# Indirect gathers issued behind TensorE's and ScalarE's work, and the first scores of an attention unit issued behind the slot's other TensorE products

## The chip, the cores and the metric

One core of a Trainium2 chip runs the whole program. The metric is device time in microseconds (us) of one execution. Before the change the median of four runs is 15278.71 us (15266.43 to 15290.21).

## The reference, cut to what matters

```
x = x + conv(gn(x))                    # two mamba layers, along time and along variables
t = tokens(x)                          # (4, 3072, 256) = 12288 tokens
n = layernorm(t)
h = tanh(q[:, :, None, :] + k[:, None, :, :] + bh)      # q, k: 32 numbers a token
e = einsum('biju,u->bij', h, Wa) + ba                   # "scores"
t = t + softmax(e) @ n                                  # attention inside each of 4 batches
n2 = layernorm(t)
g = n2 @ W_gat                                          # 4 heads x 4 experts
a_src, a_dst = (g * att_src).sum(-1), (g * att_dst).sum(-1)
alpha = softmax over each token's incoming edges of leaky_relu(a_src[src] + a_dst[dst])
s = layernorm(segment_sum(g[src] * alpha, dst))         # gates: top 2 of 4 experts
t = t + sum over experts e of gate_e * (gelu(n2 @ W1[e] + b1[e]) @ W2[e] + b2[e])
```

The edge list has 1048576 entries, given as indices up to 65535. Of these only the ones that point at a real token count; the kernel sorts them out itself and then fetches the rows of their sources and targets from two tables in device memory (`tab_s`, 20 numbers a row, and `tab_a`, 4 numbers a row).

## The kernel before, in words

**Engines and order.** The kernel writes out by hand the order of the instructions of TensorE (PE), ScalarE (ACT), VectorE (DVE) and GpSimd (POOL). Each of these runs its own list strictly in that order and waits where an input or a buffer is not ready. DMAs are issued by SyncE (SP), except the indirect gathers, which POOL issues.

**Layer 0.** `Layer0.run` (L566 on) yields twice a slot, 48 slots a block of 384 columns. In each slot it emits decays on ACT (L384), scans on DVE (L401), products with the output matrix C on POOL (L408, L415 to L417), and for the next block the TensorE products px (L214), pd (L262), pt (L283) and pz (L458). These products share one PSUM buffer, `pp`; a product can start when VectorE has read the one before it out.

**Attention.** `Attention.units` (L778 on) runs interleaved with it, one slot at a time. Each slot emits one tanh over 3072 keys (L814; 3072 of them in all, into one of three `th` buffers), lets the other work emit its first half, emits the scores of the tanh of two slots before (L787), lets the other work emit its second half, and then does one step of the tail of the unit before. Eight slots make a unit of 32 queries; the eight score calls of a unit add into one PSUM buffer `pe`. After the eighth, VectorE takes the maximum (`nb`, L868) and ScalarE the exponential (`pr`, L875), which frees `pe`. The first scores of the next unit (k = 0) therefore wait for `pr`. The steps of the unit's tail follow in the next slots: two transposes (L882) and the values (L891); every fourth unit also a `spread` on POOL (`sf`, L950) and a product `together` (L955).

**Beside attention.** `steps` in `whole` gives out the second stream: layer 0 while it lasts (with some expert work in `Beside`, L1522 and L1533), then `Edges.sort` on VectorE with its TensorE products `pc` (L1216), then `Experts.early` (L1608 and L1616). When the sort has ended, two gathers of `tab_a` rows a slot are issued (`Edges.gather`, L1037) for the first three of four batches: 324 gathers of 128 rows.

**Tail.** `tail` (L1709 on) runs when attention is over. It is a list of steps t. Three steps make one expert unit (512 tokens, one expert): products `ph` (L1608), four gelus (L1690), products `po` (L1616). 37 units remain there. Among the steps stand the 36 groups of 12 edge columns: `Graph.gather` (432 gathers of `tab_s`, L1314, and the last 108 of `tab_a`), `scores` (L1331 to L1335), `spread` (L1350, L1354) and `place` (products `pa`, L1364). Group m has its scores at step 10 + 5m/2, its places up to four steps later. After the last group of a batch `finish` turns the sums into gates. Each of the 24 kept blocks of 512 tokens is then weighted and stored, at least four steps apart and not before its batch's `finish` (`half`: 16 additions on VectorE, L1693; `all`, 2 MB, `y` and `out`, 0.5 MB each, by SP).

These lines of `tail` set the steps:

```
t = G0 + PART * m // 2
at(max(0, t - 10), lambda j=j: gr.gather(j))
at(t, lambda j=j: gr.scores(j))
```

The buffers that matter: `gs` 4, `h1` (gelu's output) 2, `ko` (a unit's output) 2, `all` and `y` 2 each.

Of the kernel before, what the change touches and what calls it, by code (L numbers as in the profile page):

```python
# [26 lines left out]
P = 128  # L27
# [32 lines left out]
G1, K1 = 8, 4  # L60
GP, GG = 12, 4
EDGE_US = 2.4
G0, PART = 10, 5
KO_BUFS = 2
SLOT_US, PRODUCT_US = 1.2, 0.11
EU, EG = 32, 2
# [572 lines left out]
class Attention:  # L639
# [4 lines left out]
    def __init__(self, ctx, tc, ident, a, x1, x2, xn2T, tab_s, tab_a):  # L644
        self.nc = nc = tc.nc
        self.ident, self.x1, self.x2, self.xn2T = ident, x1, x2, xn2T
        self.tab_s, self.tab_a = tab_s, tab_a
        pool = lambda name, bufs, **k: ctx.enter_context(
            tc.tile_pool(name=name, bufs=bufs, side="right", **k))
        const = self.const = pool("atc", 1)  # L650
        self.rows, self.th, self.wk = pool("atr", 2), pool("atb", TH_BUFS), pool("atw", 1)
        self.ps_e = pool("ate", PE_BUFS, space=PSUM)
        self.ps_v = pool("atv", PV_BUFS, space=PSUM)

        def load(name, shape, ap):
# [24 lines left out]

        self.later = []

    def psum(self, name):
        return self.ps_v.tile([P, JB], F32, tag="pv", name=name)
# [90 lines left out]
    def units(self, side):  # L775
# [24 lines left out]
        while i < B * PER + LAG or todo or self.later:  # L800
# [10 lines left out]
            if b < B:  # L811
                s = self.state[b]
                th = self.th.tile([P, TOK], F32, tag="th", name="th")
                nc.scalar.activation(th, s["krep"], AF.Tanh, bias=s["qsel"][:, col:col + 1])  # L814
                behind.append(th)
            yield
            late, self.later = self.later, []
            for f in late:
                f()
            busy = tail = None  # L820
            if behind and i >= LAG:
                n, k = divmod(i - LAG, NK)
                if k == 0:
                    pe = self.ps_e.tile([P, 2, JB], F32, tag="pe", name="pe")
                scores(pe, k, behind.pop(0))
                if k == NK - 1:
                    tail = self.unit_tail(*divmod(n, TOK // QU), pe)
                    busy = True

            self.extra = 0.0 if tail or not todo else getattr(todo[0], "us", 0.0)  # L830
            yield
            if tail:

                for f in todo:
                    f()
                todo = tail()
            elif todo and hasattr(todo[0], "us"):
                if not todo[0].full:
                    beside()
                todo.pop(0)()  # L840
                busy = True
            elif todo:
                todo.pop(0)()
# [167 lines left out]
class Edges:  # L1011
# [3 lines left out]

    def __init__(self, ctx, tc, a):
        self.nc, self.tc, self.a, self.todo = tc.nc, tc, a, []
        keep = ctx.enter_context(tc.tile_pool(name="el", bufs=1))  # L1020
        new = lambda name, shape, dt=F32: keep.tile(shape, dt, tag=name, name=name)
        self.cnt = new("cnt", [P, NH])
        self.lost = new("lost", [P, 1])
        self.si, self.di = new("si", [P, 4, CQ], I32), new("di", [P, 4, CQ], I32)
        self.lane, self.tile = new("lane", [P, 4, CQ]), new("tile", [P, 4, CQ])
        self.lanes, self.tiles = new("lanes", [P, P]), new("tiles", [P, NH])
        self.nc.sync.dma_start(self.lanes, a["lanes"])

    def places(self, pool, tab_a):

        self.gd = pool.tile([P, 4, CQ, HEADS], F32, tag="gd", name="gd")
        self.tab_a, self.have = tab_a, set()

    def gather(self, q, c):
        if (q, c) not in self.have:
# [57 lines left out]
    def sort(self):  # L1093
# [4 lines left out]
        with ExitStack() as ctx:  # L1098
# [73 lines left out]
            v.tensor_scalar(hi, flat(x3), 7, None, ALU.logical_shift_right)  # L1172
            v.tensor_copy(flat(self.lane), lo)
            v.tensor_copy(flat(self.tile), hi)
            yield 1.5


# [11 lines left out]
            v.tensor_copy(l4, self.lanes.unsqueeze(2).to_broadcast([P, P, K1]))  # L1189
            v.tensor_copy(t4, self.tiles.unsqueeze(2).to_broadcast([P, NH, K1]))  # L1190
            yield 1.0
            p = ctx.enter_context(tc.tile_pool(name="eo", bufs=3))
            ps = ctx.enter_context(tc.tile_pool(name="ep", bufs=1, space=PSUM))
            pc = ps.tile([P, NH], F32, tag="pc", name="pc")
            starts = [q * W2 + g for q in range(4) for g in range(0, C1, G1)]

            def one_hots(c0):
                hot = []
                for name, table, of, n in (("ol", l4, lane, P), ("oh", t4, tile, NH)):
                    t = p.tile([P, G1 // K1, n, K1], BF16, tag=name, name=name)  # L1200
                    which = of[:, c0:c0 + G1].rearrange("p (g k) -> p g k", k=K1)
                    v.tensor_tensor(t, table.unsqueeze(1).to_broadcast([P, G1 // K1, n, K1]),
                                    which.unsqueeze(2).to_broadcast([P, G1 // K1, n, K1]),
# [1 line left out]
                    hot.append(t)  # L1205
                return hot

            ahead = one_hots(starts[0])
            yield G1 * (P + NH) / 1800
            for i in range(len(starts)):  # L1210
                hot, ahead = ahead, one_hots(starts[i + 1]) if i + 1 < len(starts) else None

                def products(i=i, hot=hot):
                    for u in range(G1):
# [13 lines left out]
class Graph:  # L1228
# [4 lines left out]
    def __init__(self, ctx, tc, a, ed, tab_s, tab_a, gates):  # L1233
# [5 lines left out]
        self.bg, self.lg, self.lb = (self.load(a, k, HF) for k in ("bg_rep", "lg_rep", "lb_rep"))  # L1239
        self.eps = self.new("eps2", [P, 1])  # L1240
        self.nc.vector.memset(self.eps, 1e-5)
        self.got, self.v, self.pa = {}, {}, {}

    def new(self, name, shape):
        return self.const.tile(shape, F32, tag=name, name=name)
# [59 lines left out]
        nc.vector.tensor_tensor(wl, wl, ed.cnt.unsqueeze(2).to_broadcast([P, NH, ROW]), ALU.mult)  # L1305
        nc.vector.tensor_tensor(acc, acc, wl, ALU.add)

    def gather(self, j):
        nc, ed = self.nc, self.ed
        gs = self.wk.tile([P, GP, ROW], F32, tag="gs", name="gs", bufs=4)  # L1310
        q, c0 = divmod(j * GP, CQ)
        rows = self.tab_s.rearrange("p n f -> (p n) f")
        for u in range(GP):
            nc.gpsimd.indirect_dma_start(  # L1314
                out=gs[:, u, :], out_offset=None, in_=rows,
                in_offset=bass.IndirectOffsetOnAxis(ap=ed.si[:, q, c0 + u:c0 + u + 1], axis=0))
            ed.gather(q, c0 + u)

        for c in range(4 * j, min(4 * j + 4, CQ)):
            ed.gather(3, c)  # L1320
        self.got[j] = gs

    def scores(self, j):
        nc = self.nc
        gs = self.got.pop(j)
        q, c0 = divmod(j * GP, CQ)
        gd = self.ed.gd[:, q, c0:c0 + GP, :]
        e = self.wk.tile([P, GP, HEADS], F32, tag="e", name="e")
# [377 lines left out]
def tail(tc, a, ed, ex, w, tab_s, tab_a, gates):  # L1706


    with ExitStack() as ctx:  # L1709
# [11 lines left out]
            at(2 * n, lambda: next(own, None))  # L1721
        hot, ready = {}, {}
        PQ = CQ // GP
        for m in range(4 * PQ):
            j = m
            t = G0 + PART * m // 2
            if m < 1:
                gr.gather(j)
            else:
                at(max(0, t - 10), lambda j=j: gr.gather(j))  # L1730
            at(t, lambda j=j: gr.scores(j))
            for g in range(GP // GG):
                at(t + 1 + g, lambda j=j, g=g: hot.update({(j, g): gr.spread(j, g)}))
                at(t + 2 + g, lambda j=j, g=g: gr.place(j, g, *hot.pop((j, g))))
# [36 lines left out]
        for t in range(max(3 * len(units) + 3, end)):  # L1771
# [3 lines left out]
            if n < len(units):  # L1775
# [9 lines left out]
                    ex.fetch(units[n + 1][0])  # L1785
                for f in ((0, 1), (2,), (3,))[part]:
                    ex.gelu(i, e, f, hs[n])
            if n and n - 1 < len(units) and part:
                i, e = units[n - 1]
                ex.outputs(i, e, hs[n - 1], 2 * (part - 1), to[n - 1], i not in kept)  # L1790
                if part == 2:
                    if i in kept:
                        ex.keep(i, e, to[n - 1])
# [100 lines left out]
def whole(tc, a, dram, out):  # L1894
# [11 lines left out]
    with ExitStack() as ctx:  # L1906
        actx, lctx, ectx = ExitStack(), ExitStack(), ExitStack()
        with tc.manual_schedule(engines={E.PE, E.Activation, E.DVE, E.Pool}):
# [10 lines left out]
            def steps():  # L1919
# [10 lines left out]
                ed = late["ed"] = Edges(ctx, tc, a)  # L1930
                ex = late["ex"] = Experts(ectx, tc, x2, xn2T, late["gates"], out, dram, l0.beside)
                lists, units, columns = ed.sort(), None, []

                us_v = us_t = 0.0
                while True:
                    us_v = min(us_v, 0.0) + EDGE_US
                    while lists and us_v > 0 and len(ed.todo) < 2:
                        us = next(lists, None)
                        if us is None:
                            lists = None  # L1940
                            pool = ectx.enter_context(tc.tile_pool(name="late2", bufs=1))
                            late["w"] = Experts.weights(pool, nc, a)
                            ed.places(pool, tab_a)
                            columns = [(q, c) for q in range(B - 1) for c in range(CQ)]
                        else:
                            us_v -= us
                    yield
# [8 lines left out]
                             if (i, e) not in ex.done], a, att.krep[B % 2])  # L1956
                    while units and us_t > 0:
                        us_t -= next(units, 1.0) or 0.0
                    for _ in range(2 if columns else 0):
                        ed.gather(*columns.pop(0))  # L1960
                    yield

# [99 lines left out]
```

## Time and profile before

| what | us |
|---|---|
| median of four runs | 15278.71 |
| the profiled execution, by its own clock | 15285.38 |
| its span, first to last instruction | 15283.6 |
| layer 0 alone, up to the first tanh | 0 to 2551 |
| attention beside layer 0 | 2551 to 11380 |
| attention beside the sort | 11380 to 12640 |
| attention beside sort's products, early experts and 324 gathers | 12640 to 14232 |
| tail | 14232 to 15284 |

In the profile's lines an engine, a line of the kernel, the tile written and the tiles read stand together; then the count, the busy time and the mean of one, and the idle time just before, with what ended it. Views by window give the busy time of each engine in a stretch and the clock that TensorE was granted (PEclk).

### The profile page before, as it was taken

What the parts mean: (1) busy time and instruction counts of PE and PEld (TensorE: products, weight loads), DVE (VectorE), ACT (ScalarE), POOL (GpSimd) and SP (SyncE); (2) the same over time, 40 slices, a digit from 0 to 9 for tenths busy, and PEclk for the clock granted to TensorE, in tenths of its full rate; (3) what the DMA queues carried; (4) which work ended last, traced back from release to release, by engine and by line L of the source; (5) the groups of instructions that cost most, each with busy time, mean ns of one, the idle gap of its engine ahead of it and who ended that gap; (6) DMA issues with size and microseconds to landing.
All of it is one profiled execution on the core that took longest, in us unless ns stands there. A gap on an engine that the chain in (4) does not pass through costs nothing.

```text
span 15283.6 us, 224326 instructions
## 1 busy us (share of the span) xinstructions
PE 11740.4 (77%) x86496; PEld 5143.0 (34%) x86496; DVE 10996.0 (72%) x15895; ACT 12175.6 (80%) x9333; POOL 8746.2 (57%) x6402
## 2 busy tenths in 40 slices
PE   5666675777777768888888777788876778888997
PEld 2222332222222233333333333333332334433554
DVE  7888888777777887777777877577768864331367
ACT  3444334999999979999999899999997889999422
POOL 4565556777777767767777677477650000026584
PEclk8888887888888888899998889999988989999999
DMA  5666665445444444454454444344541000011234
GB/s 192 204 205 203 201 202 167 148 149 156 152 150 151 158 155 147 150 154 151 149 153 152 153 149 152 111 153 151 152 134 39 20 16 12 9 30 24 63 93 147
DMA packets 1209113, 2007.86 MB, mean 131 GB/s; under 512 B 412384, under 2 KB 655712, under 8 KB 1204960
## 3 DMA queue, kind: packets, MB, share of 16 engines
q1 hardware_dynamic: 1180384, 1988.07, 40.7%
q0 software_dynamic: 27648, 5.36, 0.8%
q8 instruction: 680, 11.14, 0.3%
q14 instruction: 401, 3.28, 0.1%
HBM read 1875.19 MB, written 117.83 MB: 130 GB/s over the span
## 4 chain that ended last, share of the span: by engine, by line
PE 20%; ACT 19%; DVE 9%; issue 4%; POOL 3%; DMA 1%; SPq 0%; DVEq 0%; ACTq 0%; POOLq 0%
ACT th L814 13%; PE pe L787 8%; PE pv L891 3%; ACT dA L384 3%; POOL gs L1314 2%; DVE h L401 1%; PE po L1616 1%; ACT pr L875 1%; PE pa L1364 1%; PE ph L1608 1%; PE ptw L882 1%; DVE go L1075 1%; PE ex L1533 1%; PE px L214 1%; PE pz L458 1%
## 5 line engine op out<-in xcount | busy, mean ns | idle before, releaser
L814 ACT ACTIVATE th<-krep,qsel 128x3072 f32<-128x3072 f32 x3072 | 8670.0, 2847 | 404.6 <-PE pe L787 386.7
L787 PE MATMUL pe<-th,wa_blk 128*32 128x384 f32 x49152 | 5049.0, 540 | 1661.9 <-ACT pr L875 1440.2
L408 POOL TENSOR_TENSOR h<-h,bC 128x768 f32<-128x768 f32 x2048 | 3753.7, 1833 | 3004.6 <-DVE h L401 2626.2
L401 DVE TENSOR_TENSOR_SCAN h<-dA,dB 128x384 f32<-128x384 f32 x4096 | 3686.8, 941 | 1032.4 <-ACT dA L384 713.2
L787 PEld LDWEIGHTS pe<-th,wa_blk 128*32 128x32 f32 x49152 | 1453.0, 116 | 4237.6 <-issue 1980.1
L392 DVE TENSOR_TENSOR dB<-bB,dtu 128x768 f32<-128x768 f32 x2048 | 1942.5, 949 | 120.2 <-DMA bB<-bc 87.8
L384 ACT ACTIVATE dA<-dt,t_A 128x380 f32<-128x380 f32 x2048 | 1127.3, 571 | 896.5 <-DVE h L401 892.2
L384 ACT ACTIVATE dA<-dt,d_A 128x372 f32<-128x372 f32 x2048 | 1102.3, 561 | 598.2 <-DVE h L401 593.6
L427 PE MATMUL py<-h,ident 128*128 128x384 f32 x2176 | 990.5, 587 | 672.8 <-POOL h L408 671.3
L415 POOL TENSOR_TENSOR h<-h 128x768 f32<-128x768 f32 x752 | 1418.4, 1886 | 53.6
L950 POOL TENSOR_SCALAR sf<-sel,f 128x32 f32<-128x32 f32 x384 | 148.4, 409 | 2253.5 <-ACT f L946 2253.5
L891 PE MATMUL pv<-xn,pT 128*32 128x257 f32 x18432 | 1112.2, 390 | 147.6 <-DVE pT L884 147.0
L884 DVE COPY pT<-ptw 128x512 f32<-128x512 f32 (+1 forms) x768 | 419.6, 546 | 713.7 <-PE ptw L882 713.4
L427 PEld LDWEIGHTS py<-h,ident 128*128 128x128 f32 x2176 | 436.3, 218 | 1237.8 <-POOL h L408 1009.0
L891 PEld LDWEIGHTS pv<-xn,pT 128*32 128x32 f32 x18432 | 582.4, 112 | 729.9 <-DVE pT L884 273.7
L417 POOL TENSOR_TENSOR y<-y,h 128x384 f32<-128x384 f32 x752 | 783.7, 1042 | 59.0
L416 POOL TENSOR_TENSOR h<-h 128x384 f32<-128x384 f32 x752 | 781.7, 1039 | 58.9
L1314 POOL DMA_INDIRECT gs<-tab_s,si x432 | 525.7, 1217 | 154.9 <-issue 148.5
L893 DVE COPY pvs<-pv 128x257 f32<-128x257 f32 x384 | 160.8, 419 | 590.2 <-PE pv L891 588.7
L882 PE MATMUL ptw<-ident,pr 128*128 128x128 f32 x2304 | 477.0, 325 | 115.7 <-DVE pT L884 45.7
L1037 POOL DMA_INDIRECT gd<-tab_a,di x432 | 436.9, 1011 | 198.9 <-issue 129.7
L868 DVE TENSOR_REDUCE nb<-pe 128x1 f32<-128x768 f32 x384 | 362.0, 943 | 249.7 <-PE pe L787 249.6
(291 smaller groups left out, 14829.7 us busy)
## 6 DMA issues: line engine op xcount, KB each, us to landing
bB<-bc SPq DMA_DIRECT2D x2048, 384.0 KB
bC<-bc SPq DMA_DIRECT2D x2048, 384.0 KB
all<-kept SPq DMA_DIRECT2D x24, 2048.0 KB
x<-x SPq DMA_DIRECT2D x144, 256.0 KB
kept<-ko SPq DMA_DIRECT2D x59, 512.0 KB
x<-x SPq DMA_DIRECT2D x192, 128.0 KB
xt<-xn2T SPq DMA_DIRECT2D x41, 512.0 KB
qsel<-xn2T SPq DMA_DIRECT2D x75, 256.0 KB
```

The lines of the kernel that those rows point to most:

```text
L384: nc.scalar.activation(inner(dA[:, :T]), inner(blk["dt"][:, e, :]), AF.Exp, scale=blk["w"]["A"][:, e, i + s:i + s + 1])
L392: nc.vector.tensor_tensor(dB, blk["bB"].pop(j), z["dtu"].unsqueeze(1).to_broadcast([P, SB, T]), ALU.mult)
L401: nc.vector.tensor_tensor_scan(h[:, s, :], z.pop(("dA", e, i + s))[:, :T], z["dB"][:, s, :], 0.0, ALU.mult, ALU.add)
L408: nc.gpsimd.tensor_tensor(h, h, blk["bC"].pop(j), ALU.mult)
L415: nc.gpsimd.tensor_tensor(h0, h0, h1, ALU.add)
L416: nc.gpsimd.tensor_tensor(h0[:, 0, :], h0[:, 0, :], h0[:, 1, :], ALU.add)
L417: nc.gpsimd.tensor_tensor(y[e], y[e], h0[:, 0, :], ALU.add)
L427: nc.tensor.matmul(z["py"], self.ident, h[:, s, :], start=(i == 0), stop=(i == DS - 1))
L787: nc.tensor.matmul(pe[q * QU:(q + 1) * QU, j, :KQ // 2], self.wa[:, k, :], th[:, c0:c0 + KQ // 2], start=(k == 0), stop=(k == NK - 1))
L814: nc.scalar.activation(th, s["krep"], AF.Tanh, bias=s["qsel"][:, col:col + 1])
L891: nc.tensor.matmul(pv[q * QU:(q + 1) * QU, :C + 1], pT[:, i, q * QU:(q + 1) * QU], s["xn"][:, q * NK + i, :], start=(i == 0), stop=(i == N ...
L1314: nc.gpsimd.indirect_dma_start(out=gs[:, u, :], out_offset=None, in_=rows, in_offset=bass.IndirectOffsetOnAxis(ap=ed.si[:, q, c0 + u:c0 + ...
```

## The change

Five edits.

1. **First scores.** In `units` the scores of k = 0 are held until the other work has emitted the second half of the slot, and are issued just before the tail's step.
2. **Gathers of `tab_a` in attention.** They start as soon as the index lists are written (`listed`, before the one-hot work of the sort), one a slot, each behind a small POOL instruction (`behind`, 128x32) that reads the slot's `th` and so waits for its tanh.
3. **Room.** For that, `gd` is allocated earlier, and the sort's one-hots use three places of its own lists in the place of a pool of three buffers each.
4. **Gathers in the tail.** `Graph.gather` becomes a generator. 14 gathers are issued at the start; then each gelu and each output of a unit gives credit for 2.75 more, behind a POOL instruction that reads what the gelu or the output wrote. A group's gathers still wait until the group four before has its scores.
5. **Steps.** `PART` goes from 5 to 6: a group's scores stand at 10 + 3m.

```
-G0, PART = 10, 5
+FIRST, RATE = 14, 2.75
+G0, PART = 10, 6
...
                 if k == 0:
                     pe = self.ps_e.tile([P, 2, JB], F32, tag="pe", name="pe")
-                scores(pe, k, behind.pop(0))
+                    held = behind.pop(0)
+                else:
+                    scores(pe, k, behind.pop(0))
...
             yield
+            if held:
+                scores(pe, 0, held)
             if tail:
...
+    def behind(self, t):
+        self.nc.gpsimd.tensor_scalar(self.pace, t, 1.0, None, ALU.add)
...
+    def gathers(self):
+        for j in range(4 * CQ // GP):
+            while j >= self.scored + 4:
+                yield False
+            gs = self.wk.tile([P, GP, ROW], F32, tag="gs", name="gs", bufs=4)
...
+            for u in range(GP):
+                nc.gpsimd.indirect_dma_start(...)
+                yield True
+                for which in [(q, c0 + u)] + [(3, c) for c in more[u // 3:u // 3 + 1] if u % 3 == 0]:
+                    if which not in ed.have:
+                        ed.gather(*which)
+                        yield True
+            self.got[j] = gs
...
+        def some(t):
+            if credit[0] is None:
+                return
+            credit[0] += RATE
+            if credit[0] >= 1:
+                ed.behind(t)
+            while credit[0] >= 1:
+                credit[0] -= 1
+                more = next(gathers, None)
...
+                if not more:
+                    credit[0] = 0.0
+        for _ in range(FIRST):
+            next(gathers)
...
                     ex.gelu(i, e, f, hs[n])
+                    some(hs[n][:, f, :QU])
...
                 ex.outputs(i, e, hs[n - 1], 2 * (part - 1), to[n - 1], i not in kept)
+                some(to[n - 1][:, 2 * part - 1, :QU])
...
-                    for _ in range(2 if columns else 0):
+                    if columns and ed.listed and att.normed > columns[0][0] and att.now:
+                        ed.behind(att.now[:, :QU])
                         ed.gather(*columns.pop(0))
```

More of the change, by code (lines that the diff above doesn't have):

```diff
@@ L679, in __init__ @@
         self.extra, self.entry, self.col, self.asked, self.normed = 0.0, 0, 0, 0, 0
-        self.later = []
+        self.later, self.now = [], None
     def psum(self, name):
@@ L815, in units @@
                 behind.append(th)
+                self.now = th
+            else:
+                self.now = None
             yield
@@ L819, in units @@
                 f()
-            busy = tail = None
+            busy = tail = held = None
             if behind and i >= LAG:
@@ L824, in units @@
                     pe = self.ps_e.tile([P, 2, JB], F32, tag="pe", name="pe")
-                scores(pe, k, behind.pop(0))
+                    held = behind.pop(0)
+                else:
+                    scores(pe, k, behind.pop(0))
                 if k == NK - 1:
@@ L1011, with __init__ @@
 class Edges:
-    def __init__(self, ctx, tc, a):
-        self.nc, self.tc, self.a, self.todo = tc.nc, tc, a, []
+    def __init__(self, ctx, tc, a, tab_a):
+        self.nc, self.tc, self.a, self.todo, self.tab_a = tc.nc, tc, a, [], tab_a
         keep = ctx.enter_context(tc.tile_pool(name="el", bufs=1))
@@ L1026, in __init__, with places @@
         self.lanes, self.tiles = new("lanes", [P, P]), new("tiles", [P, NH])
+        self.pace, self.listed = new("pace", [P, QU]), False
+        self.have = set()
         self.nc.sync.dma_start(self.lanes, a["lanes"])
-    def places(self, pool, tab_a):
+    def places(self, pool):
         self.gd = pool.tile([P, 4, CQ, HEADS], F32, tag="gd", name="gd")
-        self.tab_a, self.have = tab_a, set()
+    def behind(self, t):
+        self.nc.gpsimd.tensor_scalar(self.pace, t, 1.0, None, ALU.add)
     def gather(self, q, c):
@@ L1174, in sort @@
             v.tensor_copy(flat(self.tile), hi)
+            self.listed = True
             yield 1.5
@@ L1191, in sort @@
             yield 1.0
-            p = ctx.enter_context(tc.tile_pool(name="eo", bufs=3))
+            places = [lists.tile([P, W1], BF16, tag=k, name=f"hot_{k}") for k in ("move", "keep", "go")]
             ps = ctx.enter_context(tc.tile_pool(name="ep", bufs=1, space=PSUM))
@@ L1195, in sort, with one_hots @@
             starts = [q * W2 + g for q in range(4) for g in range(0, C1, G1)]
-            def one_hots(c0):
+            def one_hots(i):
                 hot = []
-                for name, table, of, n in (("ol", l4, lane, P), ("oh", t4, tile, NH)):
-                    t = p.tile([P, G1 // K1, n, K1], BF16, tag=name, name=name)
+                c0, place = starts[i], places[i % len(places)]
+                for o, table, of, n in ((0, l4, lane, P), (G1 * P, t4, tile, NH)):
+                    t = place[:, o:o + G1 * n].rearrange("p (g n k) -> p g n k", n=n, k=K1)
                     which = of[:, c0:c0 + G1].rearrange("p (g k) -> p g k", k=K1)
@@ L1206, in one_hots @@
                 return hot
-            ahead = one_hots(starts[0])
+            ahead = one_hots(0)
             yield G1 * (P + NH) / 1800
             for i in range(len(starts)):
-                hot, ahead = ahead, one_hots(starts[i + 1]) if i + 1 < len(starts) else None
+                hot, ahead = ahead, one_hots(i + 1) if i + 1 < len(starts) else None
                 def products(i=i, hot=hot):
@@ L1241, in __init__ @@
         self.nc.vector.memset(self.eps, 1e-5)
-        self.got, self.v, self.pa = {}, {}, {}
+        self.got, self.v, self.pa, self.scored = {}, {}, {}, 0
     def new(self, name, shape):
@@ L1306, in own_edges @@
         nc.vector.tensor_tensor(acc, acc, wl, ALU.add)
-    def gather(self, j):
+    def gathers(self):
         nc, ed = self.nc, self.ed
-        gs = self.wk.tile([P, GP, ROW], F32, tag="gs", name="gs", bufs=4)
-        q, c0 = divmod(j * GP, CQ)
         rows = self.tab_s.rearrange("p n f -> (p n) f")
[L1313 to L1321, printed above, removed]
+        for j in range(4 * CQ // GP):
+            while j >= self.scored + 4:
+                yield False
+            gs = self.wk.tile([P, GP, ROW], F32, tag="gs", name="gs", bufs=4)
+            q, c0 = divmod(j * GP, CQ)
+            more = list(range(4 * j, min(4 * j + 4, CQ)))
+            for u in range(GP):
+                nc.gpsimd.indirect_dma_start(
+                    out=gs[:, u, :], out_offset=None, in_=rows,
+                    in_offset=bass.IndirectOffsetOnAxis(ap=ed.si[:, q, c0 + u:c0 + u + 1], axis=0))
+                yield True
[4 more added lines that the diff above has]
+            self.got[j] = gs
     def scores(self, j):
         nc = self.nc
-        gs = self.got.pop(j)
+        gs, self.scored = self.got.pop(j), j + 1
         q, c0 = divmod(j * GP, CQ)
@@ L1723, in tail, with scores @@
         PQ = CQ // GP
+        gathers, credit = gr.gathers(), [0.0]
+        def scores(j):
+            while j not in gr.got:
+                next(gathers)
+            gr.scores(j)
+        def some(t):
[7 more added lines that the diff above has]
+                more = next(gathers, None)
+                if more is None:
+                    credit[0] = None
+                    return
+                if not more:
+                    credit[0] = 0.0
+        for _ in range(FIRST):
+            next(gathers)
         for m in range(4 * PQ):
@@ L1726, in tail @@
             t = G0 + PART * m // 2
[L1727 to L1731, printed above, removed]
+            at(t, lambda j=j: scores(j))
             for g in range(GP // GG):
@@ L1929, in steps @@
                 late["gates"] = keep.tile([P, NH, NEXP], F32, tag="gates", name="gates")
-                ed = late["ed"] = Edges(ctx, tc, a)
+                ed = late["ed"] = Edges(ctx, tc, a, tab_a)
                 ex = late["ex"] = Experts(ectx, tc, x2, xn2T, late["gates"], out, dram, l0.beside)
-                lists, units, columns = ed.sort(), None, []
+                ed.places(ectx.enter_context(tc.tile_pool(name="late1", bufs=1)))
+                lists, units = ed.sort(), None
+                columns = [(q, c) for q in range(B - 1) for c in range(CQ)]
                 us_v = us_t = 0.0
@@ L1942, in steps @@
                             late["w"] = Experts.weights(pool, nc, a)
-                            ed.places(pool, tab_a)
-                            columns = [(q, c) for q in range(B - 1) for c in range(CQ)]
                         else:
```

## The prediction

> **What bounds the kernel now.** I read the page first, then busy time by stage, then ACT's waits by stage, then the trace around one unit's first scores, then POOL's order in the tail.
>
> ```profile
> span 15283.6 us, 224326 instructions
> L814 ACT ACTIVATE th<-krep,qsel 128x3072 f32<-128x3072 f32 x3072 | 8670.0, 2847 | 404.6 <-PE pe L787 386.7
> L787 PE MATMUL pe<-th,wa_blk 128*32 128x384 f32 x49152 | 5049.0, 540 | 1661.9 <-ACT pr L875 1440.2
> ```
>
> The tanh is the costliest group and waits 386.7 us in all for scores, since it has three buffers. PE waits 1440.2 us for `pr`, 3.75 us at each of 384 units: this is the gap that edit 1 wants to fill.
>
> ```profile
> 2551.00:11380.00 8829.00, 6889.21 (x57157) 2858.47 (x57160) 6706.08 (x9433) 8413.51 (x6283) 6260.54 (x4489) 0.89 0.47 149
> 11380.00:12640.00 1260.00, 923.00 (x8629) 390.61 (x8622) 974.91 (x1583) 1011.08 (x415) 26.31 (x42) 0.88 0.09 29
> 12640.00:14232.00 1592.00, 1391.99 (x14250) 629.11 (x14248) 487.07 (x948) 1533.19 (x630) 334.45 (x388) 0.94 0.08 19
> 14232.00:15284.00 1052.00, 932.07 (x2884) 542.52 (x2876) 679.59 (x1238) 236.90 (x293) 656.08 (x546) 0.95 0.39 109
> ```
>
> The columns are length, then busy PE, PEld, DVE, ACT, POOL, then clock, DMA share, GB/s. Attention is bound by ACT (95% busy beside layer 0), the tail by PE (932 of 1052). What ACT loses in attention:
>
> ```profile
> ACT th L814 <- PE pe L787: 184.2, 219, 4.3
> ACT dA L384 <- DVE h L401: 154.9, 157, 7.4
> ```
>
> So beside layer 0 edit 1 can win at most 184 us, and 202 us after it by the same view. Stages below are priced in that order.
>
> **Edit 1 beside layer 0.** The built order of the changed kernel shows what passes in front of the 384 first scores: 136 units of this stage have a product there, the others nothing. Unit by unit in the trace I took the wait W of the first scores, the product's time D, when its inputs were ready (last VectorE read of its PSUM buffer), and the slack up to the tanh that needs the first `th` buffer back.
>
> ```profile
> 7541.28 0.88 ACT L875 ACTIVATE pr<-pe,nb 128x768 f32<-128x768 f32 x1
> 7542.06 2.84 ACT L814 ACTIVATE th<-krep,qsel 128x3072 f32<-128x3072 f32 x1
> 7542.21 1.50 PE L787 MATMUL pe<-th,wa_blk 128*32 128x384 f32 x16 [0.37 <-ACT pr L875]
> 7543.64 2.91 PE L458 MATMUL pz<-xin,d_in_z 128*128 128x384 f32 x4
> 7545.31 2.84 ACT L814 ACTIVATE th<-krep,qsel 128x3072 f32<-128x3072 f32 x1
> ```
>
> Here pz's buffer is free only 0.2 us after the first scores begin. Put first, pz runs to 7545.3 and the scores to 7546.8, but the tanh of 7545.31 needs them: a new stall of 1.5 us. By product: ex (L1533, 25 units) is ready 1.6 us or more before, saves 1.6 each where a later stall exists, +32 us. pt (L283, 21 units) +12. pz (L458, 38) loses 45, px (L214, 36) 28, the other ex (L1522, 8) 11, po (8) 0. Net 40 lost. Some of the lost time would have been waited for `dA` anyway (154.9 above), so I take +25 us; bounds -89 (every product ready, min of W, D and the unit's tanh stalls summed) to +84 (nothing saved).
>
> The Trainium skill, "TensorE: Matmul & The Clock Gate", Part 1, says that PE falls to half clock after an idle window of about 3.4 us and needs about as much work to recover. The rows agree in part: first scores take 2.79 us after waits of about 4 us and 1.50 after 0.4 us. Where pz and px wait for their buffer the idle time grows, so by that rule it is their products that run slow, and the sum stays.
>
> **Edit 1 after layer 0.** 63 units have pc, ph or po moved, inputs ready long before. Min of W, D and stalls: pc 21, ph 10, po 14, together 45; I take -42 us (bounds -45 to 0).
>
> **Edit 2.** 324 pace instructions and gathers, one a slot of 3.07 us (1592 us over 519 tanhs). A gather takes 0.95 and a gap of 0.30, a pace 0.34 (rows below): 1.6 a slot, and POOL is otherwise idle. `sf` now stands behind a pace that waits for the tanh of its slot, some 3 us later, and `together` waits for it: about 10 tiles lie in those slots, I take +5 us (0 to 20). That the old bursts go wins nothing: ACT lost 26 us from 13554 to 14232. Edit 3 keeps three buffers: nothing.
>
> **Edits 4 and 5.** The rows of the tail:
>
> ```profile
> 14395.50 0.94 POOL L1314 DMA_INDIRECT gs<-tab_s,si  x1 [0.30 <-issue]
> 14395.61 2.16 DVE L1354 TENSOR_TENSOR rh<-oh,v 128x1920 f32<-128x1920 f32 x1
> 14396.74 1.84 POOL L1314 DMA_INDIRECT gs<-tab_s,si  x1 [0.30 <-issue]
> 14398.57 2.16 DVE L1354 TENSOR_TENSOR rh<-oh,v 128x1920 f32<-128x1920 f32 x1
> 14398.89 2.66 POOL L1314 DMA_INDIRECT gs<-tab_s,si  x1 [0.30 <-issue]
> ...
> 14248.34 1.36 POOL L950 TENSOR_SCALAR sf<-sel,f 128x32 f32<-128x32 f32 x4 [88.51 <-ACT f L946]
> 14299.12 0.39 POOL L1280 PARTITION_ALL_REDUCE topa<-top  x1 [5.91 <-issue]
> ```
>
> A gather is 0.94 us alone and up to 2.9 beside the VectorE product rh. POOL is never free: groups 3 to 27 are gathered from 14344.9 to 14931.5, 384 gathers at 1.53 us, 24.4 us a group. PE needs 14.4 us a unit (two x16 of po at 3.62, 16 of ph at 7.2) and 10.1 a group (three pa x8 at 3.38). Before, 1.2 groups go with a unit: PE 26.6, POOL 29.3 a unit. PE lost 33 us between 14550 and 14960. After, one group goes with a unit: PE 24.6, POOL 24.4 plus six paces.
>
> A pace reads `h` or `ko`, which have two buffers. So gelu of unit n + 2 now waits until POOL has passed the last pace of unit n (the built order shows that wait at the first gelu of 35 of the 37 units). Behind that gelu on ACT stand the exponentials of the groups, and PE has four `ph` banks. POOL's queue thus becomes the clock of the units. A pace costs 0.34 (1.36 / 4) plus the change-over: 0.20 to 0.52 in all, by whether the gather's 0.30 gap stays or comes twice; I take 0.36, the middle. Before the last pace of unit 26 stand 423 gathers and 159 paces. POOL starts them at 14306: `topa` ends at 14299.5 and a library load follows, priced as the 5.9 idle before `topa`. 14306 + 423 x 1.53 - 5 (the first three groups ran at 1.44) + 159 x 0.36 = 15005: there gelu of unit 28 begins. By PE alone it would be 14296 + 28 x 14.4 + 24 x 10.1 + 0 to 33 idle = 14942 to 14975.
>
> From unit 28 on 9 units and 12 groups remain, 130 + 122 us, and 12 idle, since the last six places have only VectorE's 3.1 us spreads and 8 us of additions beside them: PE ends at 15269 (before: 15222.4).
>
> ```profile
> 15239.33 0.38 SPq L1697 DMA_DIRECT2D out<-y  x1
> 15249.51 0.38 SPq L1697 DMA_DIRECT2D out<-y  x1
> 15259.16 0.38 SPq L1697 DMA_DIRECT2D out<-y  x1
> ```
>
> After PE's end come, before, the last six blocks, one every 9.9 us: 61 us to the end of the span. With `PART` 6 the last place is at step 119, behind the units (113), so `finish` (20 us of VectorE and ACT) comes after PE too: 79 us. End at 15348 against 15283.6: +64 us (+39 to +90 by the price of a pace).
>
> The Trainium skill, "SBUF — State Buffer", Who interferes with whom, says that a VectorE instruction with two SBUF inputs blocks a GpSimd one that reads SBUF, whichever comes second. It speaks against the paces: they read SBUF, and rh covers 6.5 of 27 us. Were none of it shared with the gathers' own stretch, a pace would cost 0.26 more, and the sum 41 us more.
>
> **Sum.** 25 - 42 + 5 + 64 = +52 on the profiled execution's 15285.4 (span 15283.6 and 1.8 around it): 15337. That execution was 6.7 above the median of the runs, so 15330.
>
> **Rivals.**
> - *The paces never bind.* If gathers lose less to rh when spread out, PE sets the units: 14958 at unit 28, end at 15301 (+17 with 79 behind PE), attention -12, time 15284: no change. For it: with 1.27 us a gather (0.95 + 0.30) POOL would need 22.5 a unit. Against it: 1.53 measured with as many rh a group.
> - *Faster: the moved products are ready.* If px and pz can start inside the wait, edit 1 wins 89 + 45; with the tail bound by PE (+17) and `sf` +5 the time is 15278.7 - 112 = 15167, with half of it lost to `dA` 15230. It decides at readiness: each 1 us by which pz and px are free earlier is worth 74 us. Against it: the reads of that buffer end 0.1 to 2.1 us after `pr` in most units.
> - *POOL can't keep one pace and gather a slot.* `sf` x4 took 4.38 us during the sort against 1.36. At that factor pace and gather need 5.1 us a slot of 3.07, and tanh, which needs its buffer back from the pace, would lose up to 324 x 2.0 = 660; at a quarter of it the time is 15495. Against it: the one-hots fill about 0.8 us of a slot.
> - *The change doesn't do what it says*: POOL is saturated, so gathers come no later than before; that is part of the forecast.
>
> **Numbers.** Forecast 0.50 (15300 to 15405), first rival 0.22 (15255 to 15310), faster 0.18 (15165 to 15240), starved tanh 0.10 (15420 up). A measurement of this kernel can tell about 0.2% (31 us) from no change. Faster: 0.18 + 0.01. Same: 0.21 of the first rival less 0.01 above, 0.02 of the forecast: 0.21. Slower: 0.60. The range leaves out the starved case and half of the faster one: 15205 to 15405.
>
> **What would show it.** Right: first gelu of a unit waits for POOL; unit 28 starts near 15005; PE ends near 15270; 79 us follow; tanh stalls rise at the third tanh after first scores with pz. Wrong: gelu waits for PE alone, gathers with gaps, or tanh's wait for scores well under 300 us in all.

## The result, and the profile after

The changed kernel takes 15312.47 us (median of 35 runs, 15295.00 to 15328.15) against 15284.65 us before (55 runs, 15266.43 to 15307.51): ratio 1.0018, 95% interval 1.0014 to 1.0023, so about 28 us slower. Its profiled execution took 15308.26 us.

The page after gives the span, the tanh, the scores and, new among the costly groups, the gelu of the tail (count, busy time and mean of one, then the idle time before and what ended most of it):

```profile
span 15306.4 us, 225317 instructions
...
L815 ACT ACTIVATE th<-krep,qsel 128x3072 f32<-128x3072 f32 x3072 | 8668.9, 2851 | 409.7 <-PE pe L788 389.9
L788 PE MATMUL pe<-th,wa_blk 128*32 128x384 f32 x49152 | 4996.1, 535 | 1193.1 <-ACT pr L884 958.9
...
L1714 ACT ACTIVATE h<-ph,b 128x512 f32<-128x512 f32 x148 | 96.6, 685 | 661.9 <-POOL pace L1047 473.8
```

PE waits 481 us less for `pr` (1440.2 before), yet the tanh waits for its scores as long as before (386.7, now 389.9). Two stages of opposite sign are hidden in that sum: 184.2 became 223.7 beside layer 0, and 202.5 became 166.2 after it. And gelu now waits 473.8 us for paces, in a stage of 1121 us.

Busy time in two of the stages, from the view by windows of after (length; PE, PEld, DVE, ACT, POOL; clock, DMA share, GB/s), cut near where before was cut:

```profile
11380.00:12640.00 1260.00, 928.98 (x8745) 389.91 (x8744) 979.12 (x1590) 1022.52 (x420) 117.89 (x171) 0.89 0.10 29
...
14232.00:15307.00 1075.00, 913.57 (x2714) 527.34 (x2712) 665.86 (x1208) 216.70 (x278) 756.05 (x750) 0.93 0.37 104
```

After layer 0 ACT does 11 us more in the same 1260 us (1011.08 before): tanhs come earlier. In the tail POOL is busy 756 us (656 before) and PE has gaps (914 of 1075; before 932 of 1052).

The stages in numbers that don't depend on a cut: I compare the start of the same tanh, counted from 0, in both traces. The first starts at 2548.6 (2551.3 before), number 2300, some 360 us after layer 0's last decay, at 11730.3 (11739.0), the last at 14185.1 (14228.1). From the last to the end of the span it is 1121.3 us (1055.5). So the span's +22.8 us is -2.7 before attention, -6.0 beside layer 0, -34.3 after it, and +65.8 in the tail.

**Beside layer 0.** ACT's waits in after's trace from 2551 to 11380 (us in all, times, longest):

```profile
ACT th L815 <- PE pe L788: 223.7, 201, 4.6
ACT dA L385 <- DVE h L402: 129.6, 137, 7.4
ACT pr L884 <- DVE nb L877: 28.5, 24, 4.2
```

The tanh's wait for scores is up by 39.5 us (184.2 before), what the prediction worked out (40). But the wait of `dA` for the scans is down by 25.3 (154.9) and that of `pr` for the maximum by 9.1 (37.6). The waits stand in for one another: ACT stalls at one place or the other. This is how one unit with pz looks, in after's trace by time:

```profile
7540.30 2.91 PE L459 MATMUL pz<-xin,d_in_z 128*128 128x384 f32 x4 [0.57 <-DVE uab L301]
...
7543.15 1.50 PE L788 MATMUL pe<-th,wa_blk 128*32 128x384 f32 x16
...
7544.71 2.86 ACT L815 ACTIVATE th<-krep,qsel 128x3072 f32<-128x3072 f32 x1 [1.46 <-PE pe L788]
```

It is the unit that the prediction worked out: pz first, scores behind it, and a new stall of 1.46 us (1.5 forecast) at the next tanh. The `pr` ahead of it begins at 7539.15, 2.1 us earlier than in the trace before (the whole of attention starts 2.7 earlier in this one); behind the stall only 0.6 us of that is left (7544.71 against 7545.31).

**Tail.** POOL's list in after's trace at unit 28, and under it ACT's in the same stretch:

```profile
14961.05 2.06 POOL L1337 DMA_INDIRECT gs<-tab_s,si  x1 [0.30 <-issue]
14963.12 0.33 POOL L1047 TENSOR_SCALAR pace<-h 128x32 f32<-128x32 f32 x1
14963.62 1.03 POOL L1337 DMA_INDIRECT gs<-tab_s,si  x1 [0.17 <-issue]
```

```profile
14963.48 1.27 ACT L1714 ACTIVATE h<-ph,b 128x512 f32<-128x512 f32 x2 [20.62 <-POOL pace L1047]
```

The pace ends at 14963.45, and 0.03 us later gelu starts, after 20.62 us of waiting. That is the first gelu of unit 28, 778 us after the last tanh; the forecast was 15005 - 14228 = 777. From its first pace to its last gather POOL is never idle for more than 0.4 us: six paces and 16 gathers take 26.6 us by the forecast's prices, and from unit 4 to unit 28 (139 to 778 us behind the last tanh) the mean distance from unit to unit is 26.6. PE ends 1039.6 us after the last tanh (forecast 15269 - 14228 = 1041) and 81.8 us follow (79). The last stores, in SP's list of after, stand some 10 us apart as before (`out` from `y` at 15260.79, 15271.28 and 15280.91).

### The profile page after: what moved, and what is told of

It reads as the page before. It is cut to its first block, busy times and chain, and to the rows that moved or that the text cites. A ratio compares the mean times of both kernels' runs of the same rounds, so it can differ in the third digit from the quotient of the medians.

```text
span 15306.4 us, 225317 instructions
## 1 busy us (share of the span) xinstructions
PE 11702.1 (76%) x86496; PEld 5115.2 (33%) x86496; DVE 11003.6 (72%) x15895; ACT 12155.1 (79%) x9327; POOL 8996.3 (59%) x6935
## 5 line engine op out<-in xcount | busy, mean ns | idle before, releaser
L815 ACT ACTIVATE th<-krep,qsel 128x3072 f32<-128x3072 f32 x3072 | 8668.9, 2851 | 409.7 <-PE pe L788 389.9
L788 PE MATMUL pe<-th,wa_blk 128*32 128x384 f32 x49152 | 4996.1, 535 | 1193.1 <-ACT pr L884 958.9
L1714 ACT ACTIVATE h<-ph,b 128x512 f32<-128x512 f32 x148 | 96.6, 685 | 661.9 <-POOL pace L1047 473.8
```

Source lines behind the costliest of these rows:

```text
L788: nc.tensor.matmul(pe[q * QU:(q + 1) * QU, j, :KQ // 2], self.wa[:, k, :], th[:, c0:c0 + KQ // 2], start=(k == 0), stop=(k == NK - 1))
```

## The experiments

Theory: attention wins some 43 us, by edit 1 after layer 0; the tail loses 66 us, because POOL's queue, made longer by paces, clocks the units. Rivals stand with each run. Times are medians, each beside before's of the same chip; "stage" numbers are from the one trace of each. The start of attention alone differs by up to 16 us between traces (first tanh 2545.8 to 2562.0), so I compare distances between tanhs.

| run | us | before | ratio (95%) |
|---|---|---|---|
| first_scores_after_layer0 | 15259.25 | 15283.60 | 0.9983 (0.9974 to 0.9992) |
| first_scores_beside_layer0 | 15276.61 | 15283.60 | 0.9995 (0.9986 to 1.0004) |
| tail_of_before | 15253.39 | 15283.60 | 0.9980 (0.9971 to 0.9989) |
| no_held_scores | 15336.85 | 15283.60 | 1.0035 (1.0021 to 1.0049) |
| tail_no_paces | 15240.78 | 15277.86 | 0.9976 (0.9967 to 0.9985) |
| paces_of_constant | 15293.36 | 15277.86 | 1.0009 (1.0000 to 1.0018) |
| steps_only | 15243.55 | 15277.86 | 0.9977 (0.9968 to 0.9986) |
| paced_part_5 | 15365.19 | 15277.86 | 1.0054 (1.0041 to 1.0068) |
| only_ready_products | 15256.62 | 15281.28 | 0.9981 (0.9972 to 0.9990) |
| only_late_products | 15310.91 | 15281.28 | 1.0018 (1.0009 to 1.0027) |
| third_sum_buffer | 15237.48 | 15281.28 | 0.9970 (0.9958 to 0.9982) |
| third_buffer_ready_products | 15207.64 | 15281.28 | 0.9952 (0.9939 to 0.9966) |

### Edit 1 alone, after layer 0 and beside it

`free` is set where the sort starts. The second run has `not self.free`.

```
-                scores(pe, k, behind.pop(0))
+                if k == 0 and self.free:
+                    held = behind.pop(0)
+                else:
+                    scores(pe, k, behind.pop(0))
...
+            if held:
+                scores(pe, 0, held)
             if tail:
```

> The kernel before with edit 1 alone, and only after layer 0 has ended (the last 64 or so units). Theory: this holds the whole gain of attention: the last tanh starts 40 to 46 us earlier than before, the tail is as long as before (1055 us from the last tanh), so the time falls by 40 to 46 us. Rival: the gain measured in attention belongs to the early gathers of tab_a behind the tanhs (edit 2), not to the first scores: then the last tanh moves by less than 10 us and the time by less than 10 us.

> The kernel before with edit 1 alone, and only while layer 0 runs (320 units, 136 of them with a product moved in front). Theory, read from the traces of before and after: nothing is won or lost, 0 +- 6 us, because what single units lose is spent out of waits of ScalarE for the scans. The forecast of the prediction for this part: 25 us slower (with bounds of 89 faster to 84 slower). Rival: the part loses some 25 us and the other edits hid it.

After layer 0: 24 us faster (12 to 40), where I expected 40 to 46 and the rival less than 10. From tanh 2300 to the last it is 2455.6 us against 2489.1 in before (-33.5; after itself has 2454.8). The other three traces that have neither edit 1 there nor edit 2 take 2481.2 to 2485.6, so against the mean of the four the gain is 29. Most of the gain of that stage is edit 1's. Beside layer 0: 7 us faster, with an interval from 21 faster to 6 slower. By traces, first tanh to number 2300: mean of eight traces with all products held 9181.5 us (9174.0 to 9187.7), of three without 9188.8 (9187.6 to 9191.0), 7 us less. The forecast of 25 us lost is out.

### The tail of before under edits 1 to 3, and the change without edit 1

```
-G0, PART = 10, 6
+G0, PART = 10, 5
...
-            at(t, lambda j=j: scores(j))
+            if m < 1:
+                gr.gather(j)
+            else:
+                at(max(0, t - 10), lambda j=j: gr.gather(j))
+            at(t, lambda j=j: gr.scores(j))
...
-                    some(hs[n][:, f, :QU])
...
-                some(to[n - 1][:, 2 * part - 1, :QU])
```

> The changed kernel with the tail of before: edits 1 to 3 stay, the gathers of the tail are issued without paces ten steps ahead and PART is 5. Theory: the gain of attention (43 us) stays, the loss of the tail (66 us) goes: 43 us faster than before, about 15242. Rival: the tail's loss comes from what attention leaves behind (its earlier end, POOL's gathers at its end), not from paces and PART: then the time stays within 10 us of the changed kernel's, about 15312.

> The changed kernel without edit 1: first scores are issued where they were. Theory: attention is as long as before or up to 5 us longer, the tail 66 us longer: 66 to 71 us slower than before, about 15352. Rival (the gain of attention is edit 2's): attention stays 43 us shorter, the time some 28 us above before, about 15312.

With the tail of before, the last tanh starts at 14186.5, the tail takes 1061.0 us, and the time is 30 us under before (43 expected). Without edit 1 the tail takes 1119.2 and the time is 53 us over before (66 to 71 expected). Gain and loss thus belong to different edits and nearly add up (edits 2 and 3 are in both runs). The last run also shows edits 2 and 3 without edit 1: tanh 2300 to the last in 2478.8 us, 10.3 less than before, but only 2 to 7 less than the other three traces just named. So the +5 that I had is not seen, and a gain is not clear of what such traces differ by. With edit 1 nothing of it is left (2454.8 against 2455.6). PE's waits for `sf`, which I had priced, are 10.6 us in all after 12640 in that trace (8 waits, 1.6 the longest), and ACT's list of that stretch names none of it: its tanhs wait 45.6 us for scores, 52.3 before.

### What in the tail costs: paces, their data, or the steps

Three kernels: no paces (`ed.behind(t)` left out, credit kept); paces that read a constant; and steps alone, which is tail_of_before with `PART` 6.

```
             credit[0] += RATE
-            if credit[0] >= 1:
-                ed.behind(t)
```

```
-                ed.behind(t)
+                ed.behind(ed.lanes[:, :QU])
```

> The changed kernel without the pace instructions of the tail (about 200 of them); the credit, the order of the gathers and PART 6 stay, so only the reading of gelu's and the outputs' tiles by POOL is gone. Theory (POOL's queue is the units' clock through gelu's two buffers): gelu's 474 us of waiting for POOL go, TensorE sets the units, the first gelu of unit 28 comes some 20 to 45 us earlier against the last tanh, 82 us still follow TensorE's end; the tail takes 1065 to 1090 us in the place of 1121 and the time is 15255 to 15285. Rival (the loss is all in the steps of PART, the paces are free): the tail stays at 1121, the time near 15312.

> The changed kernel with all paces of the tail kept, but each reads a constant tile in the place of what a gelu or an output wrote: they take POOL's time, and no tile of the units waits for them. Theory (the buffers carry the loss): the tail takes 1070 to 1095 us, a little over that without paces, since POOL is up to 75 us later with the gathers and has about three groups in hand. Rival (POOL's time alone is the loss: gathers and paces fill it, and the groups' places wait for their gathers whatever the paces read): 1115 to 1125 us as in the changed kernel.

> Edits 1 to 3 with the gathers of the tail as before (no paces, ten steps ahead), and PART 6 in the place of 5. Theory: only finish moves behind TensorE's end: 80 us from there to the end in the place of 61, TensorE itself ends up to 5 us earlier; the tail takes 1070 to 1085 us (1061 with PART 5), the time is 15260 to 15270. Rival (PART 6 lets TensorE run without waiting for gathers, and wins back what the end costs): 1050 to 1061 us, 15240 to 15253.

| from the last tanh, us | to unit 28 | to POOL's last `gs` gather | to PE's end | tail |
|---|---|---|---|---|
| before | 799 | 869.5 | 994.3 | 1055.5 |
| after | 778 | 963.2 | 1039.6 | 1121.3 |
| tail_no_paces | 705 | 888.1 | 972.0 | 1053.0 |
| paces_of_constant | 745 | 973.5 | 1025.8 | 1107.6 |
| steps_only | 705 | 887.8 | 974.6 | 1056.8 |

Without paces the loss is gone: 1053.0 us, less than the 1065 to 1090 that I expected. The 209 paces delay POOL's last gather by 963.2 - 888.1 = 75.1 us. Of these, 11.6 are idle once, before the first pace (`POOL pace L1047 <- issue: 11.6, 1, 11.6` in after's list of waits). Without paces the gather in that place follows after 0.2 us. The rest is 0.30 us a pace, where the prediction took 0.36.

And `PART` 6 costs nothing. I expected 1070 to 1085 us from steps_only; 1056.8 is the rival's range. Against tail_of_before (PE's end at 1000.5) PE ends 26 us earlier, and 82.2 us follow in the place of 60.5. ACT's waits for `e`, the scores of gathered rows, in the tail up to PE's end, before and then steps_only (a row without a tile is the load of the exponential's table), the largest row of each:

```profile
ACT L1258 <- DVE e L1335: 215.9, 22, 21.6
```

```profile
ACT v L1275 <- DVE e L1352: 52.6, 14, 15.6
```

With the exponential's other row it is 283.8 us before and 66.9 in steps_only. With the old steps groups were asked for before their gathers were there, without any pace. PE's waits for `rh` and `ko` fall with this, from 53.4 us in tail_of_before to 33.2.

The run with constant paces is a miss of mine too. I expected 1070 to 1095 us, since nothing of the units waits for such paces any more; it is 1107.6. ACT's longest wait in the tail of that kernel but the one of gelu for its products (474.8 us):

```profile
ACT v L1275 <- DVE e L1359: 198.9, 26, 15.6
```

And the same row without paces (574.7 us of gelu for its products there):

```profile
ACT v L1275 <- DVE e L1359: 52.8, 14, 15.6
```

Gelu waits for no pace there, but the exponentials of the groups wait 199 us for `e` (53 without paces). So about 55 of the 68 us (1107.6 and 1121.3, both against 1053.0) are POOL's time, whatever the paces read (the medians of these two runs, on one chip, are 53 us apart): the units stand behind groups whose gathers are late. Only some 14 us are the wait through gelu's buffers. The line "gelu waits 473.8 us for the pace" names the place where the queue is met first, not how much taking that place away would give back.

### Paces with the old steps

The changed kernel with `G0, PART = 10, 5`.

> The changed kernel with PART 5 in the place of 6: the paces stay. Theory: POOL's queue clocks the units harder (18 gathers a unit), all its gathers and paces end near 15153, four units and some places follow, TensorE ends near 15230, and with finish in front of that 61 us remain: a tail of about 1107 us, time about 15293. Rival (only the order of the end costs): a tail of 1061 us, time about 15245.

87 us slower than before, with a tail of 1175.7 us, 69 more than I had worked out. POOL's waits first and ACT's second, in this kernel's tail:

```profile
POOL pace L1047 <- ACT h L1714: 55.4, 12, 7.6
```

```profile
ACT L1275 <- DVE e L1359: 309.4, 22, 27.3
...
ACT h L1714 <- POOL pace L1047: 135.7, 12, 22.3
ACT v L1275 <- DVE e L1359: 115.6, 11, 23.2
```

I had counted POOL's queue as running without a stop. Here it stops: a pace waits for a gelu, that gelu stands on ACT behind an exponential of a group, and that waits for gathers that stand on POOL behind the pace before. With 18 gathers wanted a unit and 16.5 credited, groups are asked for before they are there, and both sides wait in turn (425 us of ACT for `e`, 55 us of POOL for gelu). Of the 425 some 295 come with the old steps alone (220.6 + 74.1 in tail_of_before, which has no paces in its tail); POOL's waits for gelu appear only here. That a pace ties the two lists into such a ring is read from these waits; no run removes the ring alone.

### Which products may pass beside layer 0

As first_scores_beside_layer0, but held scores are issued ahead of px and pz (first run) or ahead of the others (second run; there the line stands before pt, po and ex):

```
             def _():
+                self.flush()
                 v["px"] = ps.tile([P, T], F32, tag="pp", name="px")
...
+                self.flush()
                 z["pz"] = ps.tile([P, T], F32, tag="pp", name="pz")
...
+        def flush():
+            if held:
+                scores(*held.pop())
```

> As first_scores_beside_layer0, but px and pz never pass in front of first scores: where one of them comes, the held scores are issued ahead of it; ex, pt and po still pass. Theory (the prediction's working by product: ex and pt are ready and win, pz and px are late and lose): tanh's wait for scores beside layer 0 falls from 184 us before (215 with all products held in front) to 140 to 155; waits of ScalarE for the scans take some of it back, so the stage is 10 to 25 us shorter than before and the time 15255 to 15270. Rival (what tanh wins is all paid back in the waits for scans, as what it lost was): the stage stays within 6 us of all products held, some 5 to 10 us shorter than before.

> The other half: held scores are issued ahead of ex, pt and po, and only px and pz pass in front of first scores. Theory: tanh's wait for scores beside layer 0 rises from 184 us to 240 to 260, the waits for scans fall by some 30 to 40, and the stage is 15 to 35 us longer than before (time 15293 to 15313). Rival (the losses are all made good by the waits for scans): the stage is within 6 us of before.

ACT's waits from 2551 to 11380 with only the ready products passing:

```profile
ACT th L825 <- PE pe L790: 163.4, 187, 4.4
ACT dA L385 <- DVE h L402: 151.0, 163, 7.4
```

And with only the late ones:

```profile
ACT th L825 <- PE pe L790: 241.1, 209, 4.4
ACT dA L385 <- DVE h L402: 133.3, 134, 7.4
```

The first is 25 us faster than before, the second 30 us slower (intervals 15 to 43 and 14 to 41). Edit 1 beside layer 0 is a sum of two halves of opposite sign. That readiness parts them is read from after's trace: where px is the last product in front of the first scores (52 units of this stage), the scores start on average 2.0 us behind the end of `pr`, and behind pz (42 units) 2.4 us; behind pt (32) it is 0.2 us, behind ex of the later line (25) 0.8. In before it is 0.1 us or less behind each of them. The tanh's wait is 21 us under before in the one (I expected 29 to 44) and 57 over it in the other (56 to 76). In the first the waits of `dA` fall by another 4; in the second `dA` gives back 22 and `pr` 14 (23.9 against 37.6). By ACT's waits the halves are thus -24 and +22. The traces' distances from the first tanh to number 2300 are -34 and +11, the medians -25 and +30; a single trace differs by such amounts, and I don't explain the rest.

### A version that beats both

third_sum_buffer is steps_only with one line changed; the other adds the `flush` of px and pz.

```
-        y = self.io.tile([P, NQ, C], F32, tag=tag, name="y")
+        y = self.io.tile([P, NQ, C], F32, tag=tag, name="y", bufs=3 if tag == "y2" else 2)
```

> As steps_only (edits 1 to 3, gathers of the tail as before, PART 6), with a third buffer for the sums of the kept blocks, whose loads wait at the end for the store of the block two before. Theory: VectorE then adds without gaps at the end: TensorE's end to the span's end falls from 82 to 72 to 76 us, the time to about 15236. Rival (the loads and stores themselves set the pace there): 82 us and 15243 stay.

> As third_sum_buffer, and px and pz don't pass in front of first scores. Theory: the stage beside layer 0 gives another 5 to 15 us: 15220 to 15230. Rival: no change against third_sum_buffer, 15236 to 15243.

With three buffers the end behind PE falls from 82.2 to 77.7 us, 4.5 us where I expected 6 to 10. VectorE's group of additions, steps_only in the stretch behind PE's end:

```profile
L1710 DVE SCALAR_TENSOR_TENSOR y<-all,gates,y 128x256 f32<-128x256 f32 x104 | 48.6, 484 | 10.9 <-DMA y<-x 8.0
```

And third_sum_buffer:

```profile
L1710 DVE SCALAR_TENSOR_TENSOR y<-all,gates,y 128x256 f32<-128x256 f32 x105 | 49.1, 484 | 7.3 <-DMA all<-kept 4.5
```

The additions now wait for `all`, which still has two buffers: the next wait in line. The 6 us between the medians of these two kernels come from two chips, and the intervals overlap, so the time doesn't show the 4.5 us by itself. The traces do: 77.7 and 77.8 us in the two kernels with three buffers, 81.0 to 82.2 in the five others with `PART` 6. The second kernel takes 15207.64 us, 74 under before on its chip and some 105 under after's median, the fastest here; against third_sum_buffer on the same chip that is 30 us, more than the 5 to 15 I expected for its stage (9147.6 us from the first tanh to number 2300, 9184.9 without the flush).

## Why the prediction was right, and where it was not

| step | forecast, us | trace of after | the edit alone, by medians or distances |
|---|---|---|---|
| start of attention | 0 | -3 | varies by 16 from trace to trace |
| edit 1 beside layer 0 | +25 | -6 | -7 |
| edit 1 after layer 0 | -42 | -34 with edit 2 | -24 (median), -29 to -34 (distance) |
| edit 2 | +5 | in the line above | -6 alone (not clear), -1 on top of edit 1 |
| edits 4 and 5 | +64 | +66 | +68 for paces, -4 for steps |
| sum | +52 | +23 | |

The medians say +28. The sum came that near because its errors are of opposite sign: it was some 32 us too high beside layer 0 and 8 to 18 us too hopeful after it. The tail's term carried it.

- **Edit 1 beside layer 0** is the mis-sized term. The working by product had the signs right: late products lose and ready ones win. That 39.5 us of new stalls at the tanh came where 40 were forecast is in part luck: each half alone was smaller than priced (21 us won where 32 + 12 - 11 = 33 were worked out for ready products, 57 lost where 45 + 28 = 73 were for pz and px), and other traces with the same products held show 31 (215.3 in first_scores_beside_layer0) and 38 (222.1 in tail_of_before). What failed is the sentence "Some of the lost time would have been waited for `dA` anyway (154.9 above), so I take +25 us". It gave back 15; the rows show 25.3 from `dA` and 9.1 from `pr`, 34 in all, and the time of the stage is even a little shorter. I read it so: while ACT stands at a tanh, VectorE goes on with scans that ACT would have waited for next.
- **Edit 1 after layer 0** held in sign, and was priced too high: 24 us by the medians, 29 to 34 by distances, where 42 were taken. ACT's waits from 11380 to the last tanh, before and then after:

```profile
ACT th L814 <- PE pe L787: 202.5, 187, 7.5
ACT pr L875 <- DVE nb L868: 89.6, 26, 16.8
```

```profile
ACT th L815 <- PE pe L788: 166.2, 142, 6.8
ACT pr L884 <- DVE nb L877: 88.9, 25, 16.0
```

The tanh waits 36 us less (21 with edit 1 alone: 181.6). ACT has a second wait here too, `pr` for the maximum, but it hardly changes. So the waits traded beside layer 0 and not here; what decides that, no run shows.
- **Edits 4 and 5** held, in size and place: unit 28 at 777 forecast and 778 measured from the last tanh, PE's end at 1041 and 1040, 79 and 81.8 us behind it. Part of that closeness is two prices that cancel: POOL stood idle 11.6 us before its first pace, where 5.9 was priced, and a pace cost 0.30, not 0.36. The mechanism is half of what I wrote: POOL's length carries the loss, and the two buffers of `h1` are only where it is met; with that wait taken away 55 of the 68 us stay.
- **The first rival** (paces never bind) was priced too high. I had unit 28 at 14958 by PE, 730 from the last tanh, and +17 us for the tail; without paces it is 705 and -2.5. The idle time that I had charged (16) was right: PE is idle 14.5 us on that way without paces. What was wrong is the price of PE's work. I had added up the lengths of rows, and they overlap, as before's rows show:

```profile
15141.65 3.62 PE L1616 MATMUL po<-w,h 128*128 128x256 f32 x16
15145.10 6.60 PE L1364 MATMUL pa<-rh,ol 128*128 128x480 f32 x16
```

The x16 of po has 3.62 us, but the next row begins 3.45 us later; so it is with pa and ph. In all I had 28 x 14.4 + 24 x 10.1 = 646 us up to unit 28, and PE is busy 621 us there without paces: that is the difference. The same prices stand in the forecast's 130 + 122 us behind unit 28; PE was busy 245 us there and idle 16, where 252 and 12 were added.
- **The rule on two-input VectorE instructions** (the Trainium skill, "SBUF — State Buffer", Who interferes with whom) speaks against paces. The rows agree: in after the 18 paces that lie beside an `rh` take 1.71 us on average, the other 191 take 0.35. But the gathers beside `rh` were then fewer, 109 against 119 without paces, and the price of a pace came out at 0.30 net, not 0.26 above 0.36.
- **Starved tanh** did not occur: from 11380 to the last one tanhs wait 2.8 us in all for paces.
- **TensorE's clock** was kept out of the sum, and stays out: the view by windows grants 0.89, 0.89, 0.95 and 0.93 in the four stages, 0.89, 0.88, 0.94 and 0.95 before.

## What to carry to other kernels

Before an instruction is moved into the gap of a waiting one, look when its own buffer and inputs are ready: the same edit won 25 us with ready products and lost 30 with late ones, and the mixture looked like nothing. A wait that an engine shows is not always a loss that can be had back at full price: where the same engine waits somewhere else in the same stage, the waits can trade, as they did beside layer 0 and not after it, so measure how much. An instruction that paces a saturated queue costs its time whatever it reads (here 0.30 us each where it read gelu's tiles, 0.36 where it read a constant, and some 11 us once before the first); pace a queue only if it has room. Busy lengths of rows that overlap are not a price: take the distance from start to start.

## What the hardware showed that I had not expected

An indirect gather on POOL is stretched beside the VectorE product `rh` (two inputs in SBUF, 2.16 us): in after 109 gathers of `gs` that lie beside `rh` take 1.96 us on average (up to 2.98), the other 323 take 1.00. The Trainium skill, "SBUF — State Buffer", Who interferes with whom, tells of a probe in which a `tensor_tensor` did not stall a DMA, and infers that this is because it takes only the shared read interface; the rows here say that the gather is held up all the same. But not beside every two-input instruction: 61 gathers beside the additions of `y` (0.48 us each) take 1.05 us, 37 beside `ol` (0.68 us) 1.04. Whether length or something else makes the difference, no run shows. I had read the stretch from three rows before, but not that it meets a quarter of these gathers, and without paces as much (1.89 us on 119 gathers there).
